# A graph network's attention layer: node-ordered columns and a split broadcast of the softmax maxima

## The chip, the cores and the metric

One core of a Trainium2 chip runs the kernel. The metric is the device time of one execution in microseconds (us). The core has five engines that matter here: TensorE (PE: matmuls; PEld is its weight load), VectorE (DVE), ScalarE (ACT), GpSimd (POOL) and SyncE (SP), which here only issues DMA transfers. Each works through its own queue in order; they wait for one another by semaphores. A name with a q (SPq, ACTq) is an engine's sequencer, where its waits and its DMA issues stand.

## What is computed

Input x holds 32 graphs (batches) of 512 nodes with 64 features; adj is one 512 x 512 matrix, symmetric, with some 1 to 2% of its entries set. Four layers follow each other, each of the form x = x + layer(relu(layernorm(x))). The change is in the last, a graph attention with 8 heads and an output attention:

```
def gat_layer(x, graph, W, b):
    h = x @ W
    s = jnp.einsum('bnd,bmd->bnm', h, h) * graph
    s = jnp.where(s == 0.0, NEG_INF, s)
    a = jax.nn.softmax(s, axis=2)
    return jnp.einsum('bnm,bmd->bnd', a, h) + b
...
cat = jnp.moveaxis(heads, 0, 2).reshape(B, N, H * D)
x = jax.nn.leaky_relu(cat, negative_slope=0.01)
out = gat_layer(x, graph, W_out, b_out)
return jax.nn.leaky_relu(out, negative_slope=0.01)
```

The scores s are symmetric in n and m. The softmax over m needs, for every node n, the maximum of its row and the sum of its exponentials.

## The kernel before

**Layout.** Node n = p C + c, with C = 4, lies on partition p in block c. A tile of 512 columns (N) holds the nodes block by block: column c 128 + p ("block order"). In node order the column would be p 4 + c. All numbers are fp32.

**Units and periods.** The layer is cut into 144 units. A Heads unit is one batch and two of its eight heads (k = 0, 1; 128 units); an Out unit is the output attention of two batches (16 units). The list `flow` fixes their order; eight Heads units and one Out unit follow each other at first, and the last eight Out units come at the end (`late`). The function `planned` (L705) writes one period of the schedule by hand: in period t unit t is at one stage, unit t-1 at the next, and so on, so each engine's queue is written out in the order of the lines L718 to L782. The names now, ahead and unit(k) mean the unit of period t, that of t+1 and that of t-k.

**A unit's way.**

1. `make_hx` (L521) transposes the normalized features into hx. `make_g` (L528), in every second period, multiplies them with each head's weight product and ScalarE copies the two results to g (L549). `features` (L489) prepares later batches on ScalarE, right behind those copies.
2. `scores` (L368): for each of four row blocks r, two matmuls into a PSUM pair s_ps, whose two buffers are shared with e_ps below.
3. `maxima` (L378): one VectorE instruction per r and k writes the masked, negated scores to p_att and their minimum to one column of `top`. The mask is flow_neg (L161).
4. `spread_out` (L390): VectorE transposes top in 32 x 32 squares (L392), and four transfers on SyncE write it to DRAM as top_row (L395), in block order. `spread_in` (L399): one transfer reads it back, broadcast to all partitions, as topb, 128 x 1024 (L401).
5. `shift` (L406): GpSimd subtracts topb from p_att, one 128 x 1024 instruction for each of r = 0, 2, 1, 3 (in period 1 VectorE does it). `exps` (L412): ScalarE's exponential, in place for even r, into e_ps for odd r. `join` (L418): VectorE adds the even block to the odd one.
6. `totals` (L432): matmuls with ones give the sums; ScalarE copies them (L443); two transfers, one from ScalarE's queue and one from SyncE's, bring them into parts (L448). `recips`, `recips_out`, `recips_in`: VectorE's reciprocal, then DRAM and back as the broadcast recb (L461, L468).
7. `values` (L421): the weighted sums av; `normalize` (L472): VectorE multiplies by recb into o_att.
8. Heads units: `y_pe`, `y_act`, `y_dve` (L551 to L576) apply the head's weights into cat; `Out.product` (L596) multiplies cat with the output weights into gT_ps, two heads a period.
9. Out units: `keep_product` (L606) copies to gT; `make_gs` (L621) scales it on GpSimd into gs, which both operands of the scores are; `make_v` (L610) transposes it to gV and forms gD; `bias` (L640), `back`, `back_dve`, `back_pool` and `store` end it.

PSUM holds two buffers for everything tagged m (hx, g, tot, y, gV and back), taken in turn. The columns of p_att, of topb, av, recb, o_att, y and cat are all nodes n; the partitions of p_att are nodes m.

Of the kernel before, what the change touches and what calls it, by code (L numbers as in the profile page):

```python
# [8 lines left out]
F32 = mybir.dt.float32  # L9
AF = mybir.ActivationFunctionType  # L10
OP = mybir.AluOpType
# [3 lines left out]
P = 128  # L15
LN_EPS = 1e-5
GAT_NEG = -9000000000000000.0
FLOW_NEG = -1e16
# [4 lines left out]
def fast_form(  # L23
# [25 lines left out]
    nc = tc.nc  # L49
    B, N, F = x.shape  # L50
    C = N // P
    H, _, D = w_heads.shape
# [3 lines left out]
    Q = P // 32  # L56

    const = ctx.enter_context(tc.tile_pool(name="const", bufs=1))
    xpool = ctx.enter_context(tc.tile_pool(name="xpool", bufs=1))
    tiny = ctx.enter_context(tc.tile_pool(name="tiny", bufs=4))  # L60
# [14 lines left out]
    adj_p = setup.tile([P, C, C, P], F32, name="adj_p")  # L75
# [37 lines left out]
    b_out2 = const.tile([P, 1], F32, name="b_out2")  # L113
# [27 lines left out]
    adj_f = adj_p.rearrange("p c k q -> p c (k q)")  # L141
    flow_neg = const.tile([P, C, N], F32, name="flow_neg")
# [15 lines left out]
    E_MAX = 5.0  # L158

    def masks():  # L160
        nc.vector.tensor_scalar(flow_neg, adj_f, 0.0, FLOW_NEG, op0=OP.is_equal, op1=OP.mult)  # L161

    root_d = const.tile([P, C], F32, name="root_d")
    urow = const.tile([P, N], F32, name="urow")
# [29 lines left out]
    def judge_rows(c):  # L194
        both, t = row_pair("edge"), row_pair("t")[:, 0]
        ok, edge = both[:, 1], both[:, 0]
        nc.vector.tensor_scalar(edge, adj_f[:, c], 0.0, None, op0=OP.not_equal)
        nc.vector.scalar_tensor_tensor(
            t, urow, root_d[:, c : c + 1], edge, op0=OP.mult, op1=OP.mult
        )  # L200
        nc.vector.tensor_tensor(t, t, adj_f[:, c], OP.subtract)
        nc.vector.scalar_tensor_tensor(t, t, -1.0, t, op0=OP.mult, op1=OP.max)
        nc.vector.scalar_tensor_tensor(
            ok, adj_f[:, c], 4e-7, t, op0=OP.mult, op1=OP.is_ge
        )
        nc.vector.scalar_tensor_tensor(
            edge, adj_t[:, c], 0.0, edge, op0=OP.not_equal, op1=OP.is_equal
        )
        nc.vector.tensor_reduce(
            sound[:, 2 + C + c : 3 + C + c], both.rearrange("p k n -> p (k n)"), AX.X, OP.min  # L210
        )

    def halves(k):
        return slice(k * F, (k + 1) * F)

    def row_pair(name):

        return pairs_of[0].tile([P, 2, N], F32, name=name, tag="row")


    acc_of, pairs_of = [], []

    def acc(name, shape):
        return acc_of[0].tile(shape, F32, name=name, tag=acc_of[1])
# [82 lines left out]
    LATE = 7  # L307
    ROOM = 6

    tops = [const.tile([P, 32], F32, name=f"top{i}") for i in range(2)]  # L310
    for t in tops:
        nc.gpsimd.memset(t, 0.0)
    ones = const.tile([P, 32], F32, name="ones32")
    nc.gpsimd.memset(ones, 1.0)

    class Pair:
# [15 lines left out]
        def make_g(self):  # L332
            pass

        def make_gs(self):
            pass

        def judge_product(self):
            pass
# [7 lines left out]
        def bias(self):  # L347
            pass
# [19 lines left out]
        def scores(self, r):  # L368
            g, x = self.terms()
            ps = ps_s.tile([P, 2, N], F32, name="s_ps", tag="s")  # L370
            self.s_ps[r] = ps
            for k in range(2):
                nc.tensor.matmul(  # L373
                    ps[:, k], lhsT=g[halves(k), r * P : (r + 1) * P], rhs=x[halves(k), :],
                    start=True, stop=True,
                )

# [10 lines left out]
                )  # L388

        def spread_out(self):  # L390
            t = tiny.tile([P, 32], F32, name="top_t")
            nc.vector.transpose(t, self.top)  # L392
            self.top_row = dram.tile([2 * C, P], F32, name="top_row")
            for q in range(Q):
                nc.sync.dma_start(  # L395
                    self.top_row[:, q * 32 : (q + 1) * 32], t[q * 32 : q * 32 + 2 * C, :]
                )

        def spread_in(self):  # L399
            self.topb = wk.tile([P, 2, N], F32, name="topb")  # L400
            nc.sync.dma_start(  # L401
                self.topb.rearrange("p k n -> p (k n)"),
                self.top_row.rearrange("(o r) p -> o (r p)", o=1).to_broadcast([P, 2 * N]),
            )

        def shift(self, r, engine):  # L406
            engine.tensor_tensor(self.p[r], self.p[r], self.topb, OP.subtract)  # L407

# [65 lines left out]
    class Heads(Pair):  # L476
# [51 lines left out]
        def make_g(self):  # L528
            if self.b % 2:
                return  # L530
            pss = [acc("g_ps", [P, N]) for k in range(2)]
            for k in range(2):
                u = self.pair[k]
                u.x = Heads.hx[u.b]
                u.hnv = Heads.hn[u.b]
                u.hdv = Heads.hd[u.b]
                nc.tensor.matmul(  # L537
                    pss[k],
                    lhsT=m2[halves(k), 2 * u.i : 2 * u.i + 2, :].rearrange(
                        "p h f -> p (h f)"  # L540
                    ),
                    rhs=u.x[halves(k), :],
                    start=True,
                    stop=True,
                )
            for k in range(2):
                u = self.pair[k]
                u.g = early.tile([P, N], F32, name="g", bufs=3)
                nc.scalar.copy(u.g, pss[k])  # L549

        def y_pe(self):  # L551
            self.y = []
# [25 lines left out]
        def terms(self):  # L578
            return self.g, self.x
# [7 lines left out]
    class Out(Pair):  # L587
# [17 lines left out]

        def keep_product(self):  # L606
            self.gT = wk.tile([P, N], F32, name="gT", bufs=LATE + 1)
            nc.scalar.copy(self.gT, self.gps)

        def make_v(self):  # L610
            ps = ps_m.tile([P, C, P], F32, name="gV_ps", tag="m")
# [9 lines left out]
        def make_gs(self):  # L621
            self.gs = wk.tile([P, N], F32, name="gs")
            nc.gpsimd.tensor_tensor(self.gs, self.gT, urow, OP.mult)

        def judge_product(self):
            nc.vector.tensor_reduce(
# [2 lines left out]
            )  # L629

        def terms(self):
            return self.gs, self.gs

        def v(self, k, j):
            return self.gV[:, j, halves(k)]
# [2 lines left out]
            return self.gD[:, j // 2, halves(k)]  # L638

        def bias(self):  # L640
            nc.scalar.activation(self.o, self.o, AF.Identity, bias=b_out2, scale=1.0)

        def back(self):
            self.ps = ps_m.tile([P, C, 2, F], F32, name="back_ps", tag="m")
# [145 lines left out]
    for b in range(0, B, 2):  # L790
        out_unit = Out(b)
        for i in range(H // 2):
            pair = [Heads(b + k, i) for k in range(2)]
            for k in range(2):
                u = pair[k]
# [22 lines left out]
    with (  # L818
# [94 lines left out]
        def project(terms, tag):  # L913
            p = ps_o.tile([P, C, 2, F], F32, name=tag, tag="po")
            for c in range(C):
                for i, (t, w) in enumerate(terms):
                    nc.tensor.matmul(  # L917
                        p[:, c],
                        lhsT=t[:, c * P : (c + 1) * P],
                        rhs=w,  # L920
                        start=(i == 0),
                        stop=(i == len(terms) - 1),
                    )
            return p
# [338 lines left out]
    setup_ctx.close()  # L1263


    pairs_of[:] = [ctx.enter_context(tc.tile_pool(name="pairs_b", bufs=H - 2))]
    pbuf = ctx.enter_context(tc.tile_pool(name="pbuf", bufs=4 * C - 2))

    wk = ctx.enter_context(tc.tile_pool(name="work_b", bufs=2))
    dram = ctx.enter_context(  # L1270
        tc.tile_pool(name="dram", bufs=4, space=bass.MemoryType.DRAM)
    )
# [579 lines left out]
```

## Time and profile before

| what | value |
|---|---|
| median of 3 runs | 2057.39 us (2053.95 to 2059.52) |
| the profiled execution: its time, its span | 2057.15 us, 2055.4 us |
| layer 3 from first maximum to the end of the span | 458.5 to 2055.4 us |
| four subtractions of one unit on GpSimd | 9.36 us |
| two maxima of one r on VectorE, mean of each | 686 ns |
| exponentials on ScalarE, mean | 1057 ns (SBUF), 1028 ns (PSUM) |
| transpose of top on VectorE | 211 ns, 144 times |
| four issues of top_row on SyncE | 1.3 to 1.6 us mostly |
| issue of topb on SyncE | 0.34 us |
| g copies on ScalarE, mean | 587 ns, 128 times |

A page lists groups of instructions by line: engine, operation, output<-inputs, shape and count, then busy time in us, mean in ns of one, and the idle time before them with what ended it. The chain of work that ended last is followed backwards from the last instruction; its pieces are given as start, length and what. In the busy time by stretch each line has the stretch, its length and then, for each engine, the busy time and the number of instructions, the granted clock and the share of DMA. A matmul in fp32 gives two records each, and neighbours overlap, so counts in the chain are of records.

### The profile page before, as it was taken

The page shows a single profiled execution, that of the slowest core. Times are in us where ns is not written, and L with a number is a line of the kernel's source. Part 1 is how long each engine was busy: PE and PEld are TensorE (multiplying, and loading weights), DVE is VectorE, ACT ScalarE, POOL GpSimd, SP SyncE. Part 2 cuts the span into 40 slices and gives each one's busy share as a digit, 9 for nine tenths or more (in the row PEclk, how much of TensorE's full clock was granted, in tenths as well). Part 3 has the DMA queues.
Part 4 walks back from the last instruction along what each step waited for, and adds up shares of the span by engine and source line. Part 5 has one row for each costly group of instructions (what it writes and reads, how often), then busy time and mean ns, then how long its engine had stood idle before and what let it go on. Part 6 is the DMA issues. An engine that isn't in the chain of part 4 may idle for free.

```text
span 2055.4 us, 32929 instructions
## 1 busy us (share of the span) xinstructions
PE 1977.7 (96%) x11038; PEld 805.5 (39%) x11038; DVE 1777.2 (86%) x4261; ACT 1221.0 (59%) x1944; POOL 1422.7 (69%) x693
## 2 busy tenths in 40 slices
PE   6999999997999999999999999999999999999995
PEld 4577766662333333333333333333333333333231
DVE  5799997768999899899989998989898898889994
ACT  3443443335666666667666667666676666665554
POOL 2000000006898989899988989898888888889996
PEclk9999999989999999999999999999999999999999
DMA  5000000002222222222222222222222222222223
GB/s 142 1 1 2 1 1 1 1 1 69 74 69 79 79 78 75 79 80 78 74 84 76 82 69 84 76 73 79 76 77 69 79 74 69 79 74 79 69 84 80
DMA packets 135780, 129.33 MB, mean 63 GB/s; under 512 B 92793, under 2 KB 98081, under 8 KB 135473
## 3 DMA queue, kind: packets, MB, share of 16 engines
q1 hardware_dynamic: 116368, 126.35, 19.5%
q10 hardware_dynamic: 18720, 0.59, 0.5%
q8 instruction: 88, 1.44, 0.3%
q0 software_dynamic: 512, 0.20, 0.1%
q14 instruction: 92, 0.75, 0.1%
HBM read 119.48 MB, written 5.37 MB: 61 GB/s over the span
## 4 chain that ended last, share of the span: by engine, by line
PE 68%; POOL 9%; DVE 9%; DMA 6%; issue 3%; ACT 3%; SPq 1%; POOLq 0%; ACTq 0%; DVEq 0%
PE s_ps L373 17%; PE av L425 16%; POOL p_att L407 9%; PE nt_ps L897 8%; PE acc L990 6%; PE tot_ps L437 4%; DVE p_att L385 4%; PE gT_ps L600 4%; PE y_ps L555 4%; PE g_ps L537 3%; DMA topb<-top_row 2%; DVE p_att L419 2%; ACT e_ps L416 1%; PE po L917 1%; DMA recb<-rec_row 1%
## 5 line engine op out<-in xcount | busy, mean ns | idle before, releaser
L407 POOL TENSOR_TENSOR p_att<-p_att,topb 128x1024 f32<-128x1024 f32 x572 | 1338.4, 2374 | 201.6 <-DMA topb<-top_row 144.2
L385 DVE CUSTOM_DVE_ANT_0 p_att<-s_ps,flow_neg 128x512 f32<-128x512 f32 x1152 | 726.8, 686 | 67.2 <-PE s_ps L373 66.2
L373 PE MATMUL s_ps<-hx,g 64*128 64x512 f32 x2048 | 518.8, 615 | 27.3 <-DVE p_att L419 25.0
L416 ACT ACTIVATE p_att<-p_att 128x1024 f32<-128x1024 f32 x288 | 304.3, 1057 | 219.7 <-POOL p_att L407 209.3
L419 DVE TENSOR_TENSOR p_att<-e_ps,p_att 128x1024 f32<-128x1024 f32 x288 | 342.4, 1200 | 66.7 <-ACT e_ps L416 65.3
L416 ACT ACTIVATE e_ps<-p_att 128x1024 f32<-128x1024 f32 x288 | 295.4, 1028 | 141.1 <-POOL p_att L407 123.3
L373 PEld LDWEIGHTS s_ps<-hx,g 64*128 64x128 f32 x2048 | 175.4, 186 | 342.2 <-DVE top L385 168.8
L425 PE MATMUL av<-p_att,hd 128*64 128x512 f32 x1024 | 269.6, 605 | 0.3 <-DVE o_att L474 0.2
L425 PE MATMUL av<-p_att,hn 128*64 128x512 f32 x1024 | 263.1, 592 | 0.0
L1066 POOL TENSOR_TENSOR x<-x,bias_b 128x512 f32<-128x512 f32 x16 | 20.3, 1276 | 282.5 <-DVE hn L839 282.5
L573 DVE SCALAR_TENSOR_TENSOR cat<-y_ps,bh,cat 128x512 f32<-128x512 f32 x256 | 179.9, 744 | 0.0
L565 ACT ACTIVATE cat<-y_ps,bh 128x512 f32<-128x512 f32 x256 | 161.7, 682 | 30.1 <-PE y_ps L555 28.4
L437 PE MATMUL tot_ps<-p_att,ones 128*32 128x512 f32 x1152 | 155.5, 604 | 4.4 <-DVE p_att L419 4.4
L555 PE MATMUL y_ps<-o_att,wh_sb 64*128 64x512 f32 x512 | 132.3, 590 | 0.0
L600 PE MATMUL gT_ps<-cat,wo_sb 128*64 128x512 f32 x512 | 131.6, 592 | 0.0
L425 PEld LDWEIGHTS av<-p_att,hn 128*64 128x64 f32 x1024 | 73.5, 137 | 146.2 <-issue 146.2
L425 PEld LDWEIGHTS av<-p_att,hd 128*64 128x64 f32 x1024 | 62.1, 136 | 165.8 <-issue 133.3
L990 PE MATMUL acc<-v,s 64*128 64x65 f32 x2048 | 123.9, 279 | 0.7 <-DVE s L976 0.4
L990 PEld LDWEIGHTS acc<-v,s 64*128 64x128 f32 x2048 | 120.9, 194 | 5.9 <-DVE o L1006 1.2
L897 PE MATMUL nt_ps<-adj_t,hn 128*128 128x512 f32 x256 | 117.0, 600 | 0.8 <-DVE hn L861 0.8
L474 DVE TENSOR_TENSOR o_att<-av,recb 128x512 f32<-128x512 f32 x144 | 94.8, 659 | 16.8 <-DMA recb<-rec_row 16.3
L549 ACT COPY g<-g_ps 128x512 f32<-128x512 f32 x128 | 69.4, 588 | 66.9 <-PE g_ps L537 66.9
(182 smaller groups left out, 1984.9 us busy)
## 6 DMA issues: line engine op xcount, KB each, us to landing
topb<-top_row SPq DMA_DIRECT2D x144, 512.0 KB
recb<-rec_row SPq DMA_DIRECT2D x288, 128.0 KB
top_row<-top_t SPq DMA_DIRECT2D x576, 1.0 KB
out_dram<-y SPq DMA_DIRECT2D x32, 128.0 KB
x<-in_x_dram SPq DMA_DIRECT2D x3, 1024.0 KB
parts<-tot ACTq DMA_DIRECT2D x144, 4.0 KB
parts<-tot SPq DMA_DIRECT2D x144, 4.0 KB
rec_row<-rec_flow SPq DMA_DIRECT2D x144, 4.0 KB
```

Source lines behind the costliest of these rows:

```text
L373: nc.tensor.matmul(ps[:, k], lhsT=g[halves(k), r * P : (r + 1) * P], rhs=x[halves(k), :], start=True, stop=True,)
L385: nc.vector.tensor_tensor_reduce(out=self.p[r][:, k], in0=ps[:, k], in1=flow_neg[:, r], scale=-1.0, scalar=BIG, op0=OP.add, op1=OP.min, ac ...
L407: engine.tensor_tensor(self.p[r], self.p[r], self.topb, OP.subtract)
L416: nc.scalar.activation(to, self.p[r], AF.Exp, scale=-1.0)
L419: nc.vector.tensor_tensor(self.p[r], self.joined, self.p[r - 1], OP.add)
L425: nc.tensor.matmul(self.av[halves(k), :], lhsT=self.v(k, j) if j % 2 else self.less_next(k, j), rhs=self.p[j][:, k], start=(j == 0), stop= ...
L437: nc.tensor.matmul(ps[q : q + 32, :], lhsT=ones, rhs=self.p[2 * e + 1][:, k], start=True, stop=True,)
L555: nc.tensor.matmul(ps, lhsT=wh_sb[halves(k), 2 * self.i + k, :], rhs=self.o[halves(k), :], start=True, stop=True,)
L573: nc.vector.scalar_tensor_tensor(self.cat[:, k], self.y[k], bh[:, h : h + 1], self.cat[:, k], op0=OP.add, op1=OP.max,)
L600: nc.tensor.matmul(self.gps[halves(k), :], lhsT=wo_sb[:, h, :], rhs=Heads.cat.pop((self.b + k, h)), start=(h == 0), stop=(h == H - 1),)
L897: nc.tensor.matmul(p, lhsT=lhs(k), rhs=adj_t[:, k, :], start=(k == 0), stop=(k == C - 1))
L990: nc.tensor.matmul(self.acc[k][:, r], lhsT=self.s[b // 2][halves(k), b % 2, r * P : (r + 1) * P], rhs=self.v[halves(k), b], start=(b == 0) ...
```

## The change

The columns of layer 3's score tiles go from block order to node order. Then top, whose partition p holds the maxima of nodes 4 p to 4 p + 3, is already one row of DRAM per k.

- flow_neg is written with its columns in node order, in four instructions of 128 x 512 for one of 128 x 2048.
- The operands of the score matmuls change places: hx (block order) gives the partitions, g (node order) the columns. g is written in node order by its two copies.
- top shrinks to eight columns; its transpose on VectorE goes, and one transfer replaces four. The runs of that transfer are four numbers long.
- topb comes in two transfers, one per k, and the subtraction of r = 0 is done in two instructions of 128 x 512.
- An Out unit turns its product back to block order in keep_product, makes a second, node-ordered copy gn of gs on ScalarE, and turns o back to block order in bias, now into a second o_att tile.
- The pool of row pairs (cat, y) has one buffer fewer.

```diff
     def masks():
-        nc.vector.tensor_scalar(flow_neg, adj_f, 0.0, FLOW_NEG, op0=OP.is_equal, op1=OP.mult)
+        for c in range(C):
+            nc.vector.tensor_scalar(
+                by_blocks(flow_neg[:, c]), adj_p[:, c], 0.0, FLOW_NEG,
+                op0=OP.is_equal, op1=OP.mult,
+            )
...
+    def by_blocks(row):
+        return row.rearrange("p (i c) -> p c i", c=C)
+
+    def in_blocks(row):
+        return row.rearrange("p (c i) -> p c i", c=C)
...
-    tops = [const.tile([P, 32], F32, name=f"top{i}") for i in range(2)]
-    for t in tops:
-        nc.gpsimd.memset(t, 0.0)
+    tops = [const.tile([P, 2 * C], F32, name=f"top{i}") for i in range(2)]
...
-                    ps[:, k], lhsT=g[halves(k), r * P : (r + 1) * P], rhs=x[halves(k), :],
+                    ps[:, k], lhsT=x[halves(k), r * P : (r + 1) * P], rhs=g[halves(k), :],
...
         def spread_out(self):
-            t = tiny.tile([P, 32], F32, name="top_t")
-            nc.vector.transpose(t, self.top)
-            self.top_row = dram.tile([2 * C, P], F32, name="top_row")
-            for q in range(Q):
-                nc.sync.dma_start(
-                    self.top_row[:, q * 32 : (q + 1) * 32], t[q * 32 : q * 32 + 2 * C, :]
-                )
+            self.top_row = dram.tile([2, N], F32, name="top_row")
+            nc.sync.dma_start(
+                self.top_row.rearrange("k (p c) -> p k c", c=C),
+                self.top.rearrange("p (k c) -> p k c", k=2),
+            )
 
         def spread_in(self):
             self.topb = wk.tile([P, 2, N], F32, name="topb")
-            nc.sync.dma_start(
-                self.topb.rearrange("p k n -> p (k n)"),
-                self.top_row.rearrange("(o r) p -> o (r p)", o=1).to_broadcast([P, 2 * N]),
-            )
+            for k in range(2):
+                nc.sync.dma_start(
+                    self.topb[:, k], self.top_row[k : k + 1].to_broadcast([P, N])
+                )
 
         def shift(self, r, engine):
-            engine.tensor_tensor(self.p[r], self.p[r], self.topb, OP.subtract)
+            if r:
+                engine.tensor_tensor(self.p[r], self.p[r], self.topb, OP.subtract)
+                return
+            for k in range(2):
+                p = self.p[r][:, k]
+                engine.tensor_tensor(p, p, self.topb[:, k], OP.subtract)
...
-                nc.scalar.copy(u.g, pss[k])
+                nc.scalar.copy(by_blocks(u.g), in_blocks(pss[k]))
...
         def keep_product(self):
             self.gT = wk.tile([P, N], F32, name="gT", bufs=LATE + 1)
-            nc.scalar.copy(self.gT, self.gps)
+            nc.scalar.copy(
+                self.gT.rearrange("p (c i) -> p i c", c=C),
+                self.gps.rearrange("p (i c) -> p i c", c=C),
+            )
...
             nc.gpsimd.tensor_tensor(self.gs, self.gT, urow, OP.mult)
+            self.gn = wk.tile([P, N], F32, name="gn")
+            nc.scalar.copy(by_blocks(self.gn), in_blocks(self.gs))
...
         def terms(self):
-            return self.gs, self.gs
+            return self.gn, self.gs
...
         def bias(self):
-            nc.scalar.activation(self.o, self.o, AF.Identity, bias=b_out2, scale=1.0)
+            o = wk.tile([P, N], F32, name="o_att")
+            nc.scalar.activation(
+                o.rearrange("p (c i) -> p i c", c=C),
+                self.o.rearrange("p (i c) -> p i c", c=C),
+                AF.Identity, bias=b_out2, scale=1.0,
+            )
+            self.o = o
...
-    pairs_of[:] = [ctx.enter_context(tc.tile_pool(name="pairs_b", bufs=H - 2))]
+    pairs_of[:] = [ctx.enter_context(tc.tile_pool(name="pairs_b", bufs=H - 3))]
```

## The prediction

> **What bounds the kernel now.** I read the page's busy times, then the busy time by stretch, the chain of work that ended last, and the timeline around that chain. Two whole-page rows first:
>
> ```profile
> PE 1977.7 (96%) x11038; PEld 805.5 (39%) x11038; DVE 1777.2 (86%) x4261; ACT 1221.0 (59%) x1944; POOL 1422.7 (69%) x693
> ...
> L407 POOL TENSOR_TENSOR p_att<-p_att,topb 128x1024 f32<-128x1024 f32 x572 | 1338.4, 2374 | 201.6 <-DMA topb<-top_row 144.2
> ```
>
> GpSimd idles 144.2 us for the broadcast that the change speeds up. That isn't the gain: the stretch of nine periods from 1066.6 to 1163.4 us (columns: length, then busy time of PE, PEld, DVE, ACT, POOL) shows who is full.
>
> ```profile
> 1066.60:1163.40 96.80, 95.77 (x462) 31.37 (x460) 87.81 (x220) 64.51 (x99) 85.70 (x41) 1.00 0.26 76
> ```
>
> TensorE has 1 us idle in 96.8; VectorE has 9, GpSimd 11. The chain gives a period without extras (start, length, what):
>
> ```profile
> 1599.94 1.00 PE tot_ps L437 x8
> 1600.94 1.92 PE s_ps L373 x8
> 1602.85 0.86 PE y_ps L555 x4
> 1603.71 3.58 PE av L425 x16
> 1607.30 0.86 PE gT_ps L600 x4
> 1608.15 1.92 PE s_ps L373 x8
> ```
>
> These add up to 10.14 us, with nothing but TensorE in them. A g pair adds 0.86, an hx, gV or back transpose 0.59 each. So TensorE's own floor for nine periods with one Out among them is 9 x 10.13 + 4 x 0.86 + 4 x 0.59 = 96.97 us. From the totals matmul at 482.3 to that at 1357.9 us are 81 periods: 875.6 us against 9 x 96.97 = 872.7, an excess of 2.9. The next 45 periods (to 1851.2; no Out among them) take 493.3. Their floor is 45/8 x (8 x 10.13 + 4 x 0.86 + 2 x 0.59) = 481.8, plus some 4.2 where hx and g meet in one period (g then takes 1.80 instead of 1.06, five or six times): 486.0, an excess of 7.3. So at most **10.2 us** of the steady part are anybody's but TensorE's. Where the chain leaves TensorE it mostly goes this way:
>
> ```profile
> 1513.68 0.22 DVE top_t L392
> ...
> 1515.20 1.18 DMA top_row<-top_t
> ...
> 1516.52 3.84 DMA topb<-top_row
> ```
>
> Between the second and the third line lie SyncE's sequencer steps; before the second, three issues of 0.29 to 0.57. From the end of the last maximum (1513.64) to GpSimd's start (1520.53) it is 6.9 us. Between 500 and 1934 us the chain passes through topb 12 times, and six times through recb, whose rows queue behind topb.
>
> **What the Trainium skill says.** "DMA: Bandwidth & Descriptors", Anatomy of one DMA, has a fixed cost of about 2 us a transfer, most of it the write receipt. The trace agrees in kind: rec_row, 4 KB, takes 1.38 us in the chain at 2038.83, and topb, 512 KB, 3.4 to 3.84. So halving a transfer saves less than half. The same page, Why a DMA increments its semaphore, says that an outer dimension of 128 is spread over 16 engines; both new transfers have one, so neither should be confined (the trace has no such split to compare). "SBUF — State Buffer", Door 1: The DMA port swizzle, has a note that SBUF works in 16-byte lines and that each access to a new line pays; every new ScalarE copy writes at a step of 16 bytes or more. No row writes so; one reads so, and it is slow:
>
> ```profile
> L236 ACT COPY adj_p<-adj_raw x2: 1125/1130/1135, 12.3 to 13.3; 128x512 f32<-128x512 f32 x2
> ```
>
> **The change, part by part.**
>
> (a) Maxima's rows. Gone per period: the transpose (0.21, with its start 0.25) and three of four issues. The old way from last maximum to topb's issue at 1516.52 is 2.9 us. New: about 0.1 to issue, then one transfer of 256 runs of 16 bytes. Nearest row: rec_row, 128 runs of 32 bytes, 1.38 from issue to the next issue; the trace's packet records have 128 such packets pass in about 0.4 us, so I add 0.4: 1.8, in all 1.9. Bounds: 1.4 (runs cost nothing) to 2.9 (no better than now). The parts issue of 0.57 between them on SyncE fits inside. Saves **1.0**. A new wait: VectorE's first maximum of the next unit but one overwrites top and so waits for the transfer's read (all of VectorE's queue behind it); with two buffers that is a period later, some 8 us after the landing: 0. VectorE gets 0.25 a period back; it has 9 us spare in nine periods, so 0 on the path.
>
> (b) Broadcast in two. recb's two quarter-megabyte-in-all transfers land 2.99 us after the second issue (chain at 2040.78). I take 2.9 for the first half of topb, against 3.84; bounds 2.6 to 3.8. The second half is issued 0.34 later (topb's issue) and lands about 4.2. GpSimd starts 0.9 earlier. On SyncE's queue the extra 0.34 stands ahead of rec_row's issue alone, which waits for VectorE's reciprocals a microsecond or two longer: 0; if not, 0.34 on recb in the six passages, 2.
>
> (c) The first subtraction in two. The 128x512 subtraction's nearest rows are 1276 ns (L1066) and 1284 (L623): 2 x 1.28 - 2.37 = +0.19 a period. It starts at 2.9, wants the second half at 4.2, and ends at 5.5 instead of 3.84 + 2.37 = 6.2. Together with (a), shift(0) ends some **1.7 us earlier** after its maximum. GpSimd's load becomes (85.7 + 1.7)/9 = 9.7 us a period, still a microsecond under TensorE's 10.76. Thus 12 x 1.7 = 20 us are on offer where only 10.2 are excess: TensorE is next. Some of that excess is not topb's (recb, a late join), so I take two thirds: **-7.0**.
>
> (d) Start. At 486.31 topb is on the chain with TensorE idle (29.6 us busy in the 40 from 460 on) and the next TensorE piece waits for GpSimd's fourth shift: -1.7. The period before begins with ScalarE's table load and VectorE's shifts, which the broadcast doesn't hold: 0. **-1.7.**
>
> (e) Tail. GpSimd works without a gap from about 1934 to 2030:
>
> ```profile
> 1943.69 1.28 POOL L623 TENSOR_TENSOR gs<-gT,urow 128x512 f32<-128x512 f32 x1
> 1944.97 9.34 POOL L407 TENSOR_TENSOR p_att<-p_att,topb 128x1024 f32<-128x1024 f32 x4
> ```
>
> Here the split costs 9 passes x 0.19 = +1.7; the two topb waits left there (0.34 and 1.63) go: -2.0; the last Out's bias writes strided and is on the chain (0.73 at 2044.59): +0.4. **+0.1.**
>
> (f) g copies, two in every second period. Unstrided 0.587 (L549); with the read's surcharge 1.13. Bounds 0.587 to 1.13, below nothing excluded since the work is the same size. I take 1.13, so +1.09 in such a period. What is queued behind on ScalarE:
>
> ```profile
> 988.23 1.07 ACT L549 COPY g<-g_ps 128x512 f32<-128x512 f32 x2 [1.07 <-PE g_ps L537]
> 989.19 1.28 ACT L511 ACTIVATE hs<-hn,root_d 128x128 f32<-128x128 f32 x4
> 990.37 1.05 ACT L416 ACTIVATE p_att<-p_att 128x1024 f32<-128x1024 f32 x1
> 991.31 0.58 ACT L443 COPY tot<-tot_ps 128x512 f32<-128x512 f32 x1
> ```
>
> This is the tightest period: no gap. tot then ends at 992.98 instead of 991.89; the second y matmul, which needs its PSUM buffer, starts at 993.09. Covered by 0.1. If not, VectorE's cat and exps(1) slip up to 0.8 before joins. 48 periods have features behind g, most with more slack: **+1.0** for all; 0 at 0.587.
>
> (g) Out's other copies, once in nine periods. gn (at most 1.2) waits on ScalarE for GpSimd's gs, 1.28 after the fourth shift; behind it are gV, hx and g copies. At 607.07 exps(3) ends at 608.1, gs at 608.3, and the hx copy starts only at 609.65: it fits. gT, o likewise: 0 in the steady part; if that cover failed, 0.5 x 16 = 8. The read of gn comes two periods later. Buffers: o_att's second tile and one pair row fewer (5; cat lives two periods, y about three) free in time: 0. Scores with swapped operands have the same shapes: 0.
>
> (h) The mask, once: 1.22 becomes 4 x 0.62 (VectorE's row of L236) = 2.5; VectorE sits idle 2.23 us soon after, while TensorE runs on: 0, else +1.3.
>
> Sum: -7.0 - 1.7 + 0.1 + 1.0 = **-7.6**. The profiled execution took 2057.15 (span 2055.4 and 1.75 around it), the median of the three is 2057.39, 0.24 more; so 2049.6.
>
> **Rivals.** *Hidden by TensorE.* If the excess is mostly recb, joins and buffer turns, or if a half's subtraction waits for both halves (then (b) and (c) turn to +0.34 + 0.19 and only (a) helps), the steady part gives 2 to 3 us and the sum is about -3.5: 2053.7. For it: TensorE's 99% in that stretch; against: 12 passages of topb. *ScalarE's strided writes.* Slower than now through one place: the g copies ahead of tot, whose PSUM buffer the y matmuls need. The slack of 1.2 us after 991.89 is used up at 1.19 a copy. At 1.5 each the second y stalls by up to 0.6 in the 48 periods with features: up to +29, less 8.6 gained: 2078; a mild 1.3 gives 48 x 0.23 = 11, 2059.5. Against: no unstrided-to-strided row exceeds 1.13. *More gain.* Nearly all excess goes, and the hx-and-g periods tighten too: -10.2 - 1.7 - 2 = -14: 2043.3.
>
> **Chances.** What a measurement here tells from no change is about 0.3%, 6.2 us. Forecast (2046 to 2051) 0.48, more gain 0.08, hidden 0.28 (2051 to 2059), strided stall 0.16, of which 0.04 stays within 0.3%. So faster 0.56, same 0.32, slower 0.12. The range runs from 2043 to 2060: it takes in the mild stall and leaves the hard one out.
>
> **What would show it.** Right: topb's wait on GpSimd falls from 144 to under 40 us; the topb issue follows the last maximum by 1.9; the first half lands a microsecond before the second; g copies between 0.6 and 1.13; nine periods near 97.0. Wrong: tot copies ending after y wants to start, g copies over 1.2, a top_row landing over 2.9, or nine-period stretches unchanged though GpSimd no longer waits.

## The result and the profile after

The changed kernel takes 2048.28 us (median of 7 runs, 2045.32 to 2051.82), the kernel before 2057.39 (7 runs, 2052.40 to 2061.03): a ratio of **0.9959 [0.9947, 0.9971]**, 8.4 us less, where 2049.6 was predicted. The profiled execution of the changed kernel took 2045.32 us, with a span of 2043.5 (before: 2057.15 and 2055.4).

From the page after, the busy times of the engines and three groups (busy time, mean ns, then the idle time ahead of them and what ended it):

```profile
PE 1980.7 (97%) x11038; PEld 811.0 (40%) x11038; DVE 1753.4 (86%) x4121; ACT 1295.2 (63%) x1960; POOL 1445.8 (71%) x834
...
L416 POOL TENSOR_TENSOR p_att<-p_att,topb 128x1024 f32<-128x1024 f32 x429 | 1008.1, 2383 | 0.0
...
L420 POOL TENSOR_TENSOR p_att<-p_att,topb 128x512 f32<-128x512 f32 x286 | 360.5, 1282 | 170.5 <-DMA topb<-top_row 140.1
...
L562 ACT COPY g<-g_ps 128x512 f32<-128x512 f32 x128 | 131.8, 1138 | 81.1 <-PE g_ps L550 81.1
```

Three things are to be seen. VectorE lost 24 us of work and ScalarE gained 74. Most of that is in the g copies, which went from 588 to 1138 ns in the mean (their busy time from 69.4 to 131.8 us); the rest is in the copies of the Out units. GpSimd's subtractions take 30 us more (1008.1 + 360.5 against 1338.4). And GpSimd still idles 140.1 us for topb, against 144.2 before, although the kernel is faster.

The same nine periods as before, between the totals matmuls of units 54 and 63 (columns as before):

```profile
1059.10:1155.70 96.60, 96.28 (x459) 31.41 (x457) 86.35 (x211) 69.96 (x102) 89.13 (x51) 1.00 0.30 78
```

TensorE's share is 99.7% after 98.9%, and the stretch is only 0.2 us shorter than the 96.80 before: seen in this stretch, hardly anything happened. All nine such stretches together went from 875.6 to 871.2 us, and the 45 periods after them from 493.3 to 489.8. The chain of work through one topb passage of the changed kernel (start, length, what) answers to the one shown of before:

```profile
1039.94 0.02 DVE top L395
...
1039.97 2.28 DMA top_row<-top
...
1042.33 3.66 DMA topb<-top_row
...
1046.12 0.55 POOL p_att L420
```

From the last maximum to GpSimd's start it is 6.2 us, where the passage before took 6.9. The transpose and three issues are gone, but the rows are now 2.3 us under way to topb's issue instead of 1.3 after the last of four issues.

**Where the time went.** The span shrank by 11.9 us. 3.3 of them lie ahead of layer 3: its first maximum comes at 455.2 us instead of 458.5, because the first matmul of the program ran at 8.9 us in this execution and at 13.1 in the profile of before. That isn't the change: two experiments on the kernel before, with the same beginning, have their first matmul at 10.2 and 9.1, and one with the beginning of the changed kernel has it at 12.6. From first maximum to first totals matmul it is 23.8 us before and 24.0 after. The steady part (126 periods) fell from 1368.9 to 1361.0, -7.9, and the tail from 204.2 to 203.3, -0.9. So the change is worth 8.6 us by the profiles, and 8.4 by the medians.

Over all 144 units (143 with GpSimd), medians in us from the traces, and the 95th percentile of the last row in brackets:

| | before | after |
|---|---|---|
| last maximum to topb's issue | 2.84 | 2.25 |
| topb's (first) issue to GpSimd's start | 3.82 | 3.84 |
| last maximum to GpSimd's start | 6.65 | 6.02 |
| last maximum to the end of shift(0), taken where the next subtraction starts | 8.96 (10.13) | 8.51 (9.33) |

### The profile page after: what moved, and what is told of

The parts are those of the page before. It is cut to its first block, busy times and chain, and to the rows that moved or that the text cites. A ratio compares the mean times of both kernels' runs of the same rounds, so it can differ in the third digit from the quotient of the medians.

```text
span 2043.5 us, 32571 instructions
## 1 busy us (share of the span) xinstructions
PE 1980.7 (97%) x11038; PEld 811.0 (40%) x11038; DVE 1753.4 (86%) x4121; ACT 1295.2 (63%) x1960; POOL 1445.8 (71%) x834
## 4 chain that ended last, share of the span: by engine, by line
PE 57%; POOL 8%; DVE 4%; DMA 4%; ACT 2%; issue 2%; ACTq 0%; SPq 0%; POOLq 0%; DVEq 0%
PE s_ps L383 20%; PE av L438 19%; POOL p_att L416 6%; PE tot_ps L450 5%; PE y_ps L568 5%; PE gT_ps L613 4%; PE g_ps L550 3%; DMA topb<-top_row 2%; DVE p_att L395 2%; POOL p_att L420 2%; DVE p_att L432 1%; DMA top_row<-top 1%; PE hx_ps L310 1%; ACT e_ps L429 1%; DVE cat L586 1%
## 5 line engine op out<-in xcount | busy, mean ns | idle before, releaser
L416 POOL TENSOR_TENSOR p_att<-p_att,topb 128x1024 f32<-128x1024 f32 x429 | 1008.1, 2383 | 0.0
L383 PE MATMUL s_ps<-g,hx 64*128 64x512 f32 x2048 | 515.3, 613 | 16.6 <-DVE p_att L432 14.5
L420 POOL TENSOR_TENSOR p_att<-p_att,topb 128x512 f32<-128x512 f32 x286 | 360.5, 1282 | 170.5 <-DMA topb<-top_row 140.1
L429 ACT ACTIVATE p_att<-p_att 128x1024 f32<-128x1024 f32 x288 | 304.8, 1059 | 173.7 <-POOL p_att L420 91.1
L383 PEld LDWEIGHTS s_ps<-g,hx 64*128 64x128 f32 x2048 | 174.8, 186 | 329.0 <-DVE top L395 173.8
L562 ACT COPY g<-g_ps 128x512 f32<-128x512 f32 x128 | 131.8, 1138 | 81.1 <-PE g_ps L550 81.1
L568 PE MATMUL y_ps<-o_att,wh_sb 64*128 64x512 f32 x512 | 137.4, 594 | 0.0
L487 DVE TENSOR_TENSOR o_att<-av,recb 128x512 f32<-128x512 f32 x144 | 99.2, 689 | 29.4 <-DMA recb<-rec_row 26.8
```

Source lines behind the costliest of these rows:

```text
L383: nc.tensor.matmul(ps[:, k], lhsT=x[halves(k), r * P : (r + 1) * P], rhs=g[halves(k), :], start=True, stop=True,)
L420: engine.tensor_tensor(p, p, self.topb[:, k], OP.subtract)
L429: nc.scalar.activation(to, self.p[r], AF.Exp, scale=-1.0)
L568: nc.tensor.matmul(ps, lhsT=wh_sb[halves(k), 2 * self.i + k, :], rhs=self.o[halves(k), :], start=True, stop=True,)
```

## The experiments

Each ran beside the kernel before on the same chip (whose medians were 2055.78, 2054.92 and 2054.88); ratios are to it, with their 95% intervals, and a gain or cost in us is the ratio's distance from 1, or from another ratio, times 2055. An interval of a ratio is about 2 to 3 us wide to each side, so differences of 2 or 3 us between two kernels are only just clear of it, or not clear. Line numbers are those of each kernel. The theory at the start was the prediction's: the broadcast arrives earlier, TensorE's floor caps what that is worth. Its rivals: that the relief of VectorE is the gain, and that one half of the change does all of it.

### The two halves alone, the rows alone

On the kernel before, topb comes in two transfers and the first subtraction is split:

```diff
+            for k in range(2):
+                nc.sync.dma_start(
+                    self.topb[:, k],
+                    self.top_row[k * C : (k + 1) * C].rearrange(
+                        "(o r) p -> o (r p)", o=1
+                    ).to_broadcast([P, N]),
+                )
...
```

> The kernel before with the broadcast in two transfers and the first subtraction in two, nothing else. If the prediction's steps (b) and (c) hold (first half lands 0.9 us sooner, shift(0) ends 0.7 sooner), 3 to 4 us faster than before, about 2053.5. If, as the traces of before and after suggest (3.82 and 3.84 us from the first issue to GpSimd's start), a half lands no sooner than the whole, GpSimd starts no earlier and pays 0.13 to 0.19 us a period more: 0 to 2 us slower than before, 2057.5 to 2059.

Measured: 0.9990 [0.9981, 0.9999], 2053.22 us. GpSimd starts 3.42 us after the first issue instead of 3.82, and shift(0) ends 0.20 earlier (8.76): some 2 us of gain, at the edge of the interval.

On the changed kernel, the reverse: one transfer of topb and whole subtractions, with the node order and the single transfer of the rows kept.

```diff
+            nc.sync.dma_start(
+                self.topb.rearrange("p k n -> p (k n)"),
+                self.top_row.rearrange("(o k) n -> o (k n)", o=1).to_broadcast([P, 2 * N]),
+            )
...
+            engine.tensor_tensor(self.p[r], self.p[r], self.topb, OP.subtract)
...
```

> The kernel after with one broadcast and one whole subtraction: the node order and the single row transfer stay. Theory of the rows: all of the gain, and the 0.13 to 0.19 us of the second subtraction come back, 2046.5 to 2048.5. Theory of the prediction, in which the halves bring 0.7 of 1.7 us: some 3 us slower than the kernel after, 2051 to 2052.

Measured: 0.9973 [0.9963, 0.9984], 2049.85 us. The rows with all that node order costs bring 5.5 us, and that is clear of the interval. The 2.9 left of 8.4 for the halves are not: this ratio's interval and the changed kernel's (0.9947 to 0.9971) overlap. That the halves alone don't do all of it is shown; that the rows alone don't is likely.

### VectorE's relief

The changed kernel with a transpose of a spare, constant 128 x 32 tile put back on VectorE behind the maxima; nothing reads it.

```diff
+            t = tiny.tile([P, 32], F32, name="top_t")
+            nc.vector.transpose(t, spare)
...
```

> The kernel after with the transpose of 128x32 put back on VectorE at its old place, of a spare tile and with no reader, so that VectorE carries its old load while the rows' path stays short. Theory of the path: 0 to 1.5 us slower than the kernel after, 2048 to 2050. Rival, that the gain was VectorE's 0.25 us a period: most of it is lost, 2054 to 2057.

Measured: 0.9949 [0.9936, 0.9962], 2044.69 us, no slower than the changed kernel's 0.9959. VectorE's 0.25 us a period was no part of the gain; that rival fell.

### What waiting for topb costs at all

On the kernel before, the subtraction becomes a product with a constant tile. The kernel leaves out the subtraction of the maxima, so its result isn't the layer's. topb is still sent, into one buffer instead of two, and read by nobody.

```diff
-            engine.tensor_tensor(self.p[r], self.p[r], self.topb, OP.subtract)
+            engine.tensor_tensor(self.p[r], self.p[r], small, OP.mult)
...
+    small = wk.tile([P, 2, N], F32, name="small", bufs=1)
+    nc.gpsimd.memset(small, 1e-8)
```

> The kernel before with the maxima's subtraction left out: GpSimd multiplies p_att by a constant tile in its place (same engine, shape and count), so that it never waits for topb, whose transfers still run; the softmax is then not that of the reference. It shows what all waiting for topb is worth. If TensorE's floor is what stops the gain (at most 10.2 us in the steady part, 2 to 4 at the start, 0 to 2 at the end), 12 to 16 us faster than before, 2041 to 2045. If the stalls of the chain come from VectorE, recb or buffer turns, 0 to 6 us faster. If far more hung on topb than the floor says, 25 us or more.

Measured: 0.9887 [0.9873, 0.9902], 2032.85 us: **23 us**, although this kernel reaches its first totals matmul 4.2 us later after its first maximum (28.0 us) than the kernel before. That late start is VectorE's: it does the four products of period 1, and they take 2.0, 3.4, 3.4 and 1.2 us, where the four subtractions took 1.22 each; GpSimd, which no longer waits, works beside all but the last. By its profile the steady part is 16.7 us shorter and the tail 8.0. The prediction's 10.2 us of excess in the steady part can't hold that. The chain of this kernel shows why. This is the period in which the Out unit is transposed back, with no wait in it:

```profile
1046.49 0.99 PE tot_ps L437 x8
1047.49 1.92 PE s_ps L373 x8
1049.41 0.59 PE back_ps L646 x4
1049.99 3.58 PE av L425 x16
1053.58 1.06 PE g_ps L537 x4
1054.64 1.78 PE s_ps L373 x8
1056.42 1.00 PE tot_ps L437 x8
```

There is neither a y matmul nor a gT product in it, 0.86 us each. The prediction gave all nine periods both. In this kernel's undisturbed rows of nine the periods are 10.13, 10.99, 10.72, 10.72, 10.99, 10.72, 10.99, 10.13 and 9.86 us, together **95.25** and not 96.97. So the first 81 periods of the kernel before exceeded their floor by 875.6 - 857.3 = 18.3 us and not by 2.9. Taking each period of the steady part against its floor gives this (us; the first nine issue less than the others, so each sum is 2.1 too low, in all four kernels alike):

| | sum of the excess | of it in periods over by less than 0.5 | periods over by more than 0.4 |
|---|---|---|---|
| before | 25.4 | 4.6 | 21 |
| after | 17.5 | 9.6 | 12 |
| without waiting, before | 8.7 | 1.9 | 9 |
| without waiting, after | 10.0 | 9.2 | 4 |

The change took large stalls away and brought many small ones.

The same edit on the changed kernel:

> The kernel after with the maxima's subtraction left out in the same way as in no_wait: GpSimd multiplies by a constant tile, one instruction per r, and topb's two transfers have no reader; the softmax is not the reference's. What is left between this and no_wait (ratio 0.9887 of before) is what the node order costs besides the path of the maxima. Theory of the copies: the strided copies on ScalarE cost some 7 to 8 us (4.5 in the periods with an Out unit among them, 3.1 in those without, read from the traces), so 2038 to 2042. Rival, that they are covered as the prediction's steps (f) and (g) have it: within 2 us of no_wait, 2031 to 2035.

Measured: 0.9915 [0.9901, 0.9929], 2037.28 us, slower than the last by 0.0028, 5.8 us: nearer to what was expected if node order has a price. So waiting for topb cost 23.2 us before. After, it costs 9.0: this kernel is 17.5 us faster than the kernel before, and the changed kernel 8.4. On this account the broadcast has gained 14.2 and node order costs 5.8. That the two leave 8.4 proves nothing: the three differences are taken from the same four times, and close whatever these are. Both kernels without waiting are 4 us late at the start, so the differences between them don't contain it. The four profiles, one execution each, give the account by place (us):

| | before | without waiting, before | after | without waiting, after |
|---|---|---|---|---|
| first maximum to first totals matmul | 23.8 | 28.0 | 24.0 | 28.0 |
| steady part | 1368.9 | 1352.2 | 1361.0 | 1353.5 |
| tail | 204.2 | 196.2 | 203.3 | 198.8 |

Waiting for topb thus cost the steady part 16.7 us before and 7.5 after, and the tail 8.0 and 4.5: the broadcast gained some 9 us in the steady part and 3.5 in the tail. Of the price of node order this pair shows only 1.3 us in the steady part and 2.6 in the tail.

In the traces of the steady part the price nevertheless has a pattern. The third and fourth of nine periods take 11.05 and 10.84 us here (11.08 and 10.84 in the changed kernel) instead of 10.72 both, and in the part without Out units one period in four takes 10.35 to 10.45 instead of 10.13, from one round to the next alike. These small stalls come to more than 1.3 us; the kernel without waiting before has nine periods over by more than 0.4 us, though, and this one four. So small stalls have in part taken the place of larger ones.

### One transfer or two, one subtraction or two

The changed kernel with one transfer of topb, but the first subtraction in two:

> The kernel after with the broadcast in one transfer, the first subtraction still in two. rows_only differs from it by the second subtraction alone, the kernel after by the second transfer alone. If two transfers help (GpSimd starts 3.84 us after the first issue in the kernel after, 4.05 in rows_only): 2 to 4 us slower than the kernel after, 2050 to 2052. If they only cost SyncE an issue: as the kernel after or up to 1 us faster, 2047 to 2048.

Measured: 0.9992 [0.9983, 1.0000], 2053.46 us. And with two transfers, but a whole first subtraction, which waits for both:

> The kernel after with two broadcast transfers and one whole subtraction, which waits for both. If the second transfer helps by itself (more requests in flight, the whole landing sooner): near the kernel after or 2 to 3 us faster, since GpSimd's second instruction goes. If it helps only because the subtraction starts on the first half: the start falls back by 0.3 to 0.7 us and it is no faster than rows_only (0.9973 of before), 2049 to 2052.

Measured: 1.0009 [1.0001, 1.0018], 2057.25 us. Its subtractions are back at 2377 ns, 572 times, and wait as before:

```profile
L415 POOL TENSOR_TENSOR p_att<-p_att,topb 128x1024 f32<-128x1024 f32 x572 | 1339.8, 2377 | 201.1 <-DMA topb<-top_row 146.0 <-ACT p_att L424 30.3 <-PE gT_ps L608 8.5
```

Together with the rows alone and the changed kernel this makes a square, in each cell the ratio, the median from the last maximum to GpSimd's start, and to shift(0)'s end, with its 95th percentile:

| | whole subtraction | subtraction in two |
|---|---|---|
| one transfer | 0.9973; 6.19; 8.50 (9.75) | 0.9992; 6.26; 8.73 (9.86) |
| two transfers | 1.0009; 6.57; 8.90 (9.76) | 0.9959; 6.02; 8.51 (9.33) |

Each half of this edit costs when it is alone: the second subtraction 3.9 us, the second transfer 7.4, where the whole lands later (GpSimd starts 6.57 us after the last maximum instead of 6.19). Together they bring 2.9 by these numbers. Only the 7.4 is well clear of the intervals. The changed kernel's second profile (after_again, below) has 5.88; 8.36 (9.36) in its cell, so a median moves by 0.15 us from one execution to the next, and 8.51 against 8.50 doesn't tell whether the middle is earlier. The late tail is alike in both, 9.33 and 9.36 against 9.75. That the tail is what counts is a reading of these numbers; no run isolates it.

### Who should pay for node order

First trial: hx written in node order instead of g. There are 32 such copies for 128, the g copies are plain again, and the score weights of Heads units are read at a step of four numbers.

```diff
+        def rows(self, x, k, r):
+            return x[halves(k), r::C]
...
-                nc.scalar.copy(by_blocks(u.g), in_blocks(pss[k]))
+                nc.scalar.copy(u.g, pss[k])
```

> The kernel after with the order turned once per batch: hx is written in node order (32 strided copies), the 128 g copies are plain again, and the Heads units' score weights are read from hx at a step of four columns. Theory of the copies: the 3 us of the Out-free periods and part of the 4.5 of the others come back, 3 to 5 us faster than the kernel after, 2042 to 2045. If g's copies cost nothing: as the kernel after, 2047 to 2049. If the weight loads suffer from the step (186 ns now), TensorE pays in every period: 8 loads of 0.1 to 0.2 more in 128 periods, 100 us or more slower unless they are hidden.

Measured: 1.0036 [1.0022, 1.0050], 2061.58 us, slower than the kernel before. The row of the weight loads, in the changed kernel and then here, shows where:

```profile
L383 PEld LDWEIGHTS s_ps<-g,hx 64*128 64x128 f32 x2048 | 174.8, 186 | 329.0 <-DVE top L395 173.8 <-DVE p_att L432 95.3 <-issue 52.6
```

```profile
L383 PEld LDWEIGHTS s_ps<-g,hx 64*128 64x128 f32 x2048 | 299.9, 310 | 252.7 <-DVE top L398 138.7 <-DVE p_att L435 63.8 <-issue 15.2
```

A load takes 310 ns instead of 186, and the floor of a plain period rises from 10.13 to 10.38 us. What ScalarE was spared, TensorE paid, and TensorE is the bound.

Second trial: everything in node order, Out too, without gn and with plain gT and o copies (the constant row urow is written in node order once).

> hx_nodes with the Out units in node order throughout: no gn, gT and o copied plainly, urow once more in node order, and all transposes and score weights of an Out unit read at a step of four columns. Theory of the copies: nearly all of the 7 to 8 us come back, 2038 to 2042. If only g's copies cost: as hx_nodes. If weight loads at a step cost TensorE, slower than the kernel after.

Measured: 1.0058 [1.0044, 1.0072], 2065.34 us. Sixteen Out units with strided weights (312 ns a load) cost no less than their copies had.

Third trial: the g copies stay strided, but stand behind the features on ScalarE instead of ahead of them.

```diff
             unit(-4).make_hx()
-            unit(-2).make_g()
             for step in range(3):
...
+            unit(-2).make_g()
```

> The kernel after with make_g written behind the features of later batches, not ahead of them: on ScalarE's queue the scaling of features then falls into the 1.1 to 1.5 us in which it idles for the g matmuls, and the strided g copies come last. Nothing is left out. Theory of the copies (the second y matmul waits for the tot copy, which stands behind g copies and features): most of the 7.6 us come back, 2040 to 2044. If the stall in these periods is another (PSUM turns of hx, gn, the joins): as the kernel after, 2046 to 2049. If the g copies themselves hold the totals' PSUM buffer too long once they are last: slower than the kernel after.

Measured: **0.9918 [0.9905, 0.9932], 2038.54 us, better than both kernels**. The changed kernel once more, on the same chip:

> The kernel after once more, beside these two and the kernel before on the same chip, so that they can be compared directly: 0.9959 of before, within 0.9947 to 0.9971.

Measured: 0.9952 [0.9939, 0.9966], 2044.80 us. The order of two steps on ScalarE is worth 6.3 us by the two medians and 7.0 by the ratios. The timeline of ScalarE shows the tight period in the changed kernel (start, length, engine, line, operation; in brackets the idle time before), and under it the y matmul on TensorE:

```profile
981.87 2.07 ACT L562 COPY g<-g_ps 128x512 f32<-128x512 f32 x2 [1.07 <-PE g_ps L550]
983.68 1.27 ACT L524 ACTIVATE hs<-hn,root_d 128x128 f32<-128x128 f32 x4
984.84 1.06 ACT L429 ACTIVATE p_att<-p_att 128x1024 f32<-128x1024 f32 x1
985.79 0.59 ACT L456 COPY tot<-tot_ps 128x512 f32<-128x512 f32 x1
...
986.30 1.25 PE L568 MATMUL y_ps<-o_att,wh_sb 64*128 64x512 f32 x4
```

and with the features first:

```profile
978.51 1.26 ACT L524 ACTIVATE hs<-hn,root_d 128x128 f32<-128x128 f32 x4
979.68 2.07 ACT L562 COPY g<-g_ps 128x512 f32<-128x512 f32 x2
981.50 1.10 ACT L429 ACTIVATE p_att<-p_att 128x1024 f32<-128x1024 f32 x1
982.48 0.59 ACT L456 COPY tot<-tot_ps 128x512 f32<-128x512 f32 x1
...
983.92 1.02 PE L568 MATMUL y_ps<-o_att,wh_sb 64*128 64x512 f32 x4
```

In the first, ScalarE idles 1.07 us for g_ps and then has the g copies, the features, an exponential and the tot copy to do; tot ends at 986.38, while y has begun at 986.30 and its second half still lacks a buffer: 1.25 us for 1.02. In the second the features fill that idle time, tot ends at 983.07, and y doesn't wait. The third and fourth of nine periods are back at 10.72 us, the steady part takes 1352.9, and its excess is 9.3 us, near the 8.7 of the kernel without waiting.

The busy time of all y matmuls, before, in the changed kernel and with the features first, shows the price at its place:

```profile
L555 PE MATMUL y_ps<-o_att,wh_sb 64*128 64x512 f32 x512 | 132.3, 590 | 0.0
```

```profile
L568 PE MATMUL y_ps<-o_att,wh_sb 64*128 64x512 f32 x512 | 137.4, 594 | 0.0
```

```profile
L568 PE MATMUL y_ps<-o_att,wh_sb 64*128 64x512 f32 x512 | 131.2, 589 | 0.0
```

A unit's two y matmuls take 1.02 us when nothing holds the second. Over the 128 Heads units they lose 1.7 us beyond that before and 6.8 in the changed kernel, 23 of the units more than 0.08 each. With the features first it is 0.6, and 0.6 also in the two trials with strided weights, whose g copies are plain; without waiting it is 0.6 before and 7.7 after. Strided g copies ahead of the tot copy thus cost 5 to 7 us at the second y matmul. Whether the swap would also help the kernel before wasn't tried; at this place it has 1.7 us to win there.

## Why the prediction was right, and where it wasn't

The time was right to 1.3 us (the prediction's own sum, 7.6 from 2057.39, gives 2049.8; its 2049.6 leaves out 0.24). The mechanism was right as well: the broadcast arrives earlier, part of that gain is paid back through the g copies, and both were named with their place. That the sizes meet so well is in part luck. The gain of the broadcast and the price of the copies were both put too low, and the two terms for the start and the tail were off by 1.9 and 1.0 in opposite directions.

- **The floor and the excess: mis-sized.** Nine periods were taken at 96.97 us; they are 95.25, since an Out unit has no y matmul and hands no gT product on. 0.86 twice, nine times over, is 15.5 us that seemed to be TensorE's own and were stalls. The excess is 25.4 us instead of 10.2, and 16.7 of it go when nothing waits for topb. The broadcast's term of 7.0, two thirds of 10.2, is some 9 us in the steady part by the profiles without waiting, and 14 in the whole kernel by their ratios. Its size came from a sum that was wrong; that it is near is luck.
- **(a) The rows: right in kind, smaller in size.** Topb's issue follows the last maximum by 2.25 us in the median (2.13 to 2.20 in the other kernels with this transfer) and not by 1.9, and is 0.6 to 0.7 earlier and not 1.0. The start of the transfer is as expected (0.03 us after the maximum), but it is followed by topb's issue after 1.6 to 1.7 us in a quarter of the units and after 2.1 to 3.0 in more than half. Its 256 packets of 16 bytes are done 1.13 us after the issue in nine of ten units, and the issue of parts, which stands between the two on SyncE, decides in only nine units. What makes the wait short or long in the others is open.
- **(b) The first half lands a microsecond sooner: wrong.** GpSimd starts 3.84 us after the issue (3.70 in the second profile), where one transfer of the layout of before took 3.82 and one of node order 4.05 and 4.10 (rows alone, one transfer). So the half comes 0.2 to 0.4 sooner than the whole of its own layout, and node order takes that away again. In the layout of before the half came 0.4 sooner (3.42), and the last packet of the two transfers came later (3.57 after the issue for 3.31). The fixed cost of about 2 us in the Trainium skill's page "DMA: Bandwidth & Descriptors" (Anatomy of one DMA), from which the prediction took that half a transfer saves less than half, is given there for transfers that GpSimd issues; SyncE's here agree in kind, as halving 512 KB saves 0.4 us of 3.8 at most. In the node-ordered kernels topb as a whole is slower: the last packet is through 3.48 to 3.60 us after the issue in one transfer and 3.98 in two. Why is open.
- **(c) The split subtraction: 0.19 a period, as taken** (two of 1.28 for one of 2.38). The second half is hardly ever late: GpSimd waits for it in 6 of 143 units, by 0.2 to 0.5 us. But shift(0) ends 0.45 earlier in the median (0.60 in the second profile), not 1.7; of the lead of (a) and (b) only the rows' 0.6 exists against the kernel before. That so small a step brings so much fits the first point: 39 of the 126 periods before lie more than 0.05 us over their floor, and not only twelve. How much of each stall it took isn't shown.
- **(d) The start, -1.7: wrong.** The passage that was meant, at 486.31 us, lies behind the totals matmuls of the first unit and ahead of those of the third. From the first maximum to the third unit's totals it takes 44.4 us for 44.2. In the changed kernel the rows are 2.7 us under way to topb's issue in this passage, and GpSimd starts 6.0 us after the last maximum, for 6.1 before: nothing was gained there.
- **(e) The tail, +0.1:** -0.9. Small in sum, but the profiles without waiting give some 3.5 us to the broadcast and 2.6 to node order in it, where +0.1 was the sum of -2.0, +1.7 and +0.4. What costs the 2.6 is open.
- **(f) The g copies: right in duration, mis-sized in effect.** They take 1.138 us in the mean, the 1.13 that was taken from the strided read. The Trainium skill's page "SBUF — State Buffer" (Door 1: The DMA port swizzle) says that accesses to a new 16-byte line pay, and the trace agrees: the size and the engine are the same, and the time nearly doubles. Its note has four fp32 as how far one can stride for free; a step of just four isn't free here. But the effect was put at 1.0 us, from one period's slack of 0.1 us that the others were supposed to exceed. The y matmuls lose 5 to 7 us to it, and the two comparisons of whole kernels give 5.8 and 6.3, the first of them not all at this place. The place was right, tot behind g and ahead of the second y; the rival of the strided stall named it and looked for it only above 1.19 a copy. It began below, and in the periods that repeat in every nine.
- **(g) and (h) Out's copies and the mask: 0, as taken.** gn takes 1.15 us, gT 1.08 and the bias 1.20, and no unit in the steady part is seen waiting for gn; the mask is four instructions of 629 ns, long before layer 3.

Of the marks that were named, the one that topb's wait on GpSimd falls from 144 to under 40 us misled most. The kernel before without waiting for topb shows it: there GpSimd idled 67.3 us ahead of its subtractions, mostly for the last maximum, and 46.0 ahead of gs. When TensorE sets the period at 10.7 us (96.6 over nine) and GpSimd has 9.9 of work in it (89.13 over nine), the rest must stand somewhere, and in the changed kernel it stands ahead of the first subtraction. That wait is the period less the work, not the loss. Where it ended, the loss did show in other rows: "ACT p_att waits for POOL p_att" fell from 208.2 to 138.6 us (91.1 behind L420 and 47.5 behind L416). The price showed as well, in the waits of the stretch from 500 us on (total, times, longest; us):

```profile
PEld tot_ps L450 <- ACT g L562: 42.4, 56, 0.8
...
DVE cat L586 <- ACT cat L578: 14.0, 21, 1.2
```

The first was 27.3 us in 36 waits before; the second is 1.7 us with the features first, while the first stays there (46.2). So it is the second that goes with the small stalls.

## What to carry to other kernels

Where a floor decides what a gain can be worth, work it out for each kind of period from what that unit really issues, and test it on the shortest periods that the trace has: a term counted once too often turns waiting into work. An idle total of an engine that isn't the bound can stay while the loss goes, 140.1 us of 144.2 here; set each period against its floor, and large and small stalls come apart. And when an instruction gets longer, look at what stands behind it in its queue before looking for a shorter form: here a swap of two steps brought back 6 to 7 us and took the stall behind the strided copies away, while sparing the copies by strided weights cost more than it brought.

## What the runs showed of the hardware

- A ScalarE copy of 128 x 512 fp32 from PSUM that writes at a step of 16 bytes takes 1.14 us in the mean, and 0.59 without the step; at a step of 512 bytes 1.08, from SBUF to SBUF 1.15. VectorE's mask at a step of 16 bytes takes 4 x 0.63 us for 1.22 in one piece.
- A weight load of 64 x 128 fp32 that reads at a step of 16 bytes takes 310 ns for 186. It is hidden in part: a plain period, with 16 such loads, grew by 0.25 us, and 16 times 124 ns are 2.0.
- A broadcast of topb in two transfers isn't two halves of it: packets of 2048 bytes take 84 ns, those of 4096 bytes 159, but the last one is through 0.3 to 0.5 us later than in one transfer, and the two issues take SyncE 0.80 us together for 0.34.
- A transfer of 256 packets of 16 bytes, 9 ns each, has its last packet done 1.13 us after the issue; the transfer that waits for it was issued 1.6 to 3.0 us after that issue in most units.
- In the two kernels without waiting, VectorE's products of 128 x 1024 fp32 took 2.0 to 3.4 us while GpSimd's ran beside them, and 1.21 us once GpSimd was done.
